# Shifted-window block and dynamic convolution on one core: the order of the projection's moving columns, its bias, and the place of the taps' product

## The chip, the cores and the metric

The kernel runs on 1 core of one Trainium2 chip, in one launch. The metric is the device time of an execution in microseconds (us); shown is the median of three runs. All tensors are float32. The engines are named as in the profile: PE is TensorE's matmul, PEld its weight load, DVE VectorE, ACT ScalarE, POOL GpSimd, SP the queue that issues most transfers.

## The reference

The input x is 16 images of 192 channels by 56 by 56. Layer 0 is a Swin block with windows of 7 by 7, a shift of 3 and 6 heads; layer 1 is a 3 by 3 depthwise convolution whose weights are computed from each image's channel means. Cut to what matters:

```
h = roll(ln(x), (-3, -3)); win = 7x7 windows of h            # 49 tokens each
q, k, v = split(win @ qkv_w + qkv_b)
attn = softmax(q * SCALE @ k.T + rel_bias + shift mask)
out = (attn @ v) @ proj_w + proj_b
x1 = x + roll(windows back to the image, (3, 3))
x2 = x1 + gelu(ln(x1) @ fc1_w + fc1_b) @ fc2_w + fc2_b
t  = relu(gamma * (mean(x2) @ w1.T - running_mean) * rsqrt(var + eps) + beta)
wt = (t @ w2.T + b2), masked to 4 of the 9 taps              # one set for each image and channel
y  = depthwise conv(x2, wt) + bias
```

## The kernel before

**Tiling.** An image is cut into four pairs of window rows. A unit s is one such pair, 14 pixel rows of one image: the upper window row lies on partitions 0 to 63 and the lower one on 64 to 127, and the 192 channels are G = 3 groups of 64. `rows(s)` is the unit's part of the tile x, [128, 3, 7 rows, 56 columns]. With 16 images there are 64 units. A window row has 8 windows of 49 tokens, UT = 392 tokens; HT = 196 is half of that, four windows.

**Stages.** The loop at L1364 makes one stage for each r and keeps several units in flight: values and scores of unit r, the weighted sum and `projection` of unit r-1, `first_layer` (FC1) of unit r-2, `second_layer` (FC2) of unit r-3, the two layer norms' `statistics` and `deviations`, and, where unit r-3 was the last of its image, `taps`. `conv` of an image follows in the stages after its taps, in six pieces. In steady state PE goes through a stage in this order, by lines: L654 values, L549 scores, L654 values, L690 weighted sum, L821 FC2, L746 and L732 projection, L469 queries and keys, L783 FC1, L318 statistics, and in every fourth stage L850, the taps' product.

**Order.** `Plan.add` records each operation with an engine, an estimated duration and the keys that it reads and writes. PE's operations keep the order in which they are added; `Plan.order` lists the other engines by earliest start and due time in its own estimates. Each engine then works through its list strictly in order, and so does SP. `bank()` hands out four PSUM tiles ps0 to ps3 in turn, so a product waits for the readers of the bank used four products earlier.

**Projection.** `broad` (L742) multiplies the heads' outputs o1 (128 channels) by `wp4`, `narrow` (L728) adds o2 (64 channels) by `wp2`. The copies at L717 and L719 leave o1 and o2 window by window, 49 tokens in a run. The moving operand is read as "p r n c": for each pixel row seven tokens of each of four windows. So the PSUM result is in pixel order, 28 columns to a row, and the sums of L770 read it in rows: for each group of channels one instruction for the first half (7 rows of 28), one for the second half without its last columns (7 of 25) and one for the 3 columns that wrap to the left edge, nine in all. Each is (psum + pbt) + x, with the projection's bias `pbt` as a scalar for each partition. `broad` uses the two column halves of the array, two matmuls side by side, and `narrow` all four quadrants. One matmul of the program is two records in the profile.

**Taps.** `taps(b)` (L835) sums up the means (`pooled`, L843), multiplies them by `w1t` with the 128 columns of a broadcast `pooled` as weights (L850, three matmuls), and on DVE makes the row of 48 (L861, L862), its products with `w2r` (L863), their sums and the bias of the taps (L876, L879).

The transfers that the text speaks of: `away` (L365) writes the inverse deviations to DRAM and L374 spreads them to `rb`; L454 (xs2) and L425 to L436 (xs1) on POOL scale x by rb for FC1 and for queries and keys; L282 loads x, L625 turns the attention shares, L948 stores y.

Of the kernel before, what the change touches and what calls it, by code (L numbers as in the profile page):

```python
# [9 lines left out]
AF = mybir.ActivationFunctionType  # L10
ALU = mybir.AluOpType
# [34 lines left out]
class Plan:  # L46
# [7 lines left out]
    def add(self, eng, dur, fn, reads=(), writes=(), lag=0.0, slack=60.0, by=None):  # L54
        i = len(self.ops)
        deps = set()
        reads, writes = flat(reads), flat(writes)
        for k in reads:
            if k in self.writer:
                deps.add(self.writer[k])  # L60
        for k in writes:
            if k in self.writer:
                deps.add(self.writer[k])
            deps.update(self.readers.get(k, ()))
        for k in reads:
            self.readers.setdefault(k, []).append(i)
        for k in writes:
            self.writer[k] = i
            self.readers[k] = []
        deps.discard(i)  # L70
        self.ops.append((eng, dur, fn, sorted(deps), lag, slack, by))
# [70 lines left out]
def tile_swin_then_dynamic_conv(  # L142
# [114 lines left out]
    def P(j):  # L257
        return slice(64 * j, 64 * j + 64)

    def X(s):  # L260

        b, u = divmod(s, NU)
        return [("x", b % 3, u, i) for i in range(3)]
# [409 lines left out]
    def weighted(s):  # L673
# [25 lines left out]
        for j in range(3):  # L699
# [8 lines left out]
            for i in range(4):  # L708
# [9 lines left out]
                else:  # L718
                    add("DVE", 0.56, lambda dst=dst, src=src: nc.vector.tensor_copy(dst, src), [k], [("o", j, i)])  # L719

    def projection(s):
        pf, kf = bank()
        pq, kq = bank()
        o1k = [("o", j, i) for j in range(2) for i in range(4)]
        o2k = [("o", 2, i) for i in range(4)]
        by_rows = "p n (r c) -> p r n c"

        def narrow():  # L728
            for m in range(G):
                for ab in range(2):  # L730
                    for i, p in ((0, pf), (1, pq)):
                        nc.tensor.matmul(  # L732
                            p[P(ab), m // 2, (m % 2) * HT : (m % 2) * HT + HT],
                            wp2[P(i), m * 64 : (m + 1) * 64],
                            o2[P(i), ab].rearrange(by_rows, c=WS),
                            start=False,
                            stop=True,
                            tile_position=(64 * i, 64 * ab),
                            skip_group_check=True,
                        )  # L740

        def broad():  # L742
            for i, p in ((0, pf), (1, pq)):
                for m in range(G):
                    for ab in range(2):
                        nc.tensor.matmul(  # L746
                            p[P(ab), m // 2, (m % 2) * HT : (m % 2) * HT + HT],
                            wp4[:, m * 64 : (m + 1) * 64],
                            o1[:, ab, 4 * i : 4 * i + 4].rearrange(by_rows, c=WS),
                            start=(m % 2 == 0),  # L750
                            stop=False,
                            tile_position=(0, 64 * ab),
                            skip_group_check=True,
                        )

        add("PE", 2.05, broad, o1k + ["wp"], [kf, kq])
        add("PE", 1.05, narrow, o2k + ["wp"], [kf, kq])
        xv = rows(s)
        hw = IMG // 2
        for p, k, c0, at, n, dur in (  # L760
            (pf, kf, 0, SHIFT, hw, 0.37),
            (pq, kq, 0, SHIFT + hw, hw - SHIFT, 0.35),
            (pq, kq, hw - SHIFT, 0, SHIFT, 0.2),
        ):
            for m in range(G):
                def go(p=p, c0=c0, at=at, n=n, m=m):
                    src = p[:, m // 2, (m % 2) * HT : (m % 2) * HT + HT]
                    src = src.rearrange("p (r c) -> p r c", c=hw)[:, :, c0 : c0 + n]
                    xs = xv[:, m, :, at : at + n]
                    nc.vector.scalar_tensor_tensor(  # L770
                        xs, src, pbt[:, m : m + 1], xs, ALU.add, ALU.add
                    )
                add("DVE", dur, go, [k, "pbt"], X(s))


    def first_layer(s):
# [58 lines left out]
    def taps(b):  # L835


        p, pk = bank()
        sl = b % 3
        add(  # L840
            "DVE",
            0.2,
            lambda: nc.vector.tensor_reduce(pooled, sums[b % 2], AX.X, ALU.add),  # L843
            [("sums", b % 2)],
            ["pooled"],
        )

        def product():
            for g in range(G):
                nc.tensor.matmul(  # L850
                    p[:, 0, 0:RED],
                    pooled[:, g : g + 1].broadcast_to([128, 128]),
                    w1t[:, g],
                    start=(g == 0),
                    stop=(g == G - 1),
                )

        add("PE", 0.3, product, ["pooled", "w1t"], [pk])

        def scale():  # L860
            nc.vector.tensor_tensor(trow, p[:, 0, 0:RED], bns, ALU.mult)  # L861
            nc.vector.tensor_tensor(trow, trow, bnb, ALU.add)  # L862
            nc.vector.scalar_tensor_tensor(  # L863
                prod,
                trow.rearrange("p (o r) -> p o r", o=1).broadcast_to([128, G * NTAP, RED]),
                0.0,
                w2r.rearrange("p g t r -> p (g t) r"),
                ALU.max,
                ALU.mult,
            )  # L870

        add("DVE", 1.2, scale, [pk, "bn", "w2r"], ["sq", "trow"])
        w = wt[b % 2].rearrange("p g t -> p (g t)")

        def fin():
            nc.vector.tensor_reduce(  # L876
                w.rearrange("p (k o) -> p k o", o=1), prod, AX.X, ALU.add
            )
            nc.vector.tensor_tensor(w, w, b2t.rearrange("p g t -> p (g t)"), ALU.add)  # L879

        add("DVE", 0.9, fin, ["sq", "b2t"], [("wt", b % 2)])
        t = xt[sl]
        for to, of, row in ((0, 1, LR), (1, 0, LR)):
            def go(to=to, of=of, row=row):
                nc.sync.dma_start(t[P(to), :, 0, :], t[P(of), :, row, :])
            add("SP", 0.65, go, X(b * NU + NU - 1), [("halo", sl, to)], lag=2.5)
# [474 lines left out]
    def has(s):  # L1361
        return 0 <= s < S

    for r in range(-2, S + 3):  # L1364
# [45 lines left out]
            turn_shares()  # L1410
        if has(r - 3):
            second_layer(r - 3)
        if has(r - 1):
            projection(r - 1)
            statistics(1, r - 1)
        if not early and has(r + 1):
            queries_keys(r + 1, (0, 1, 2))
        if has(r - 2):
# [2 lines left out]
            table("natural_log_exp_and_others")  # L1421
        if norms:
            deviations(norms)
        b, k = divmod(r - 3, NU)
        if k == NU - 1 and 0 <= b < B:
            taps(b)
        for b in range(B):
            k = r - (b * NU + NU + 3)
            if b == B - 1 and r == S + 2:
# [85 lines left out]
```

## Time and profile before

| what | value |
|---|---|
| median of 3 runs | 2835.39 us (2834.74 to 2842.21) |
| profiled execution: time | 2838.8 us |
| profiled execution: span | 2837.0 us |
| granted TensorE clock, mean | 0.99 |
| PE busy | 2771.9 us, 98% of the span |
| DVE, ACT, POOL busy | 1857.8, 1562.2, 1605.6 us |
| L746 (broad), L732 (narrow) busy | 153.1 us, 84.2 us |
| L770 (the sums) busy | 576 instructions, 156.1 us by the page |
| L850 (taps' product) busy | 13.9 us, 96 records |

Busy time of a matmul line is the time in which at least one of its records ran; single records overlap, so the mean of a record (347 ns for L746) is longer than its share. The start of a record minus the start of the one before it in the same part of the array is the pace. A releaser is the operation that ended a wait.

### The profile page before, as it was taken

What the parts mean: (1) busy time and instruction counts of PE and PEld (TensorE: products, weight loads), DVE (VectorE), ACT (ScalarE), POOL (GpSimd) and SP (SyncE); (2) the same over time, 40 slices, a digit from 0 to 9 for tenths busy, and PEclk for the clock granted to TensorE, in tenths of its full rate; (3) what the DMA queues carried; (4) which work ended last, traced back from release to release, by engine and by line L of the source; (5) the groups of instructions that cost most, each with busy time, mean ns of one, the idle gap of its engine ahead of it and who ended that gap; (6) DMA issues with size and microseconds to landing.
All of it is one profiled execution on the core that took longest, in us unless ns stands there. A gap on an engine that the chain in (4) does not pass through costs nothing.

```text
span 2837.0 us, 79158 instructions
## 1 busy us (share of the span) xinstructions
PE 2771.9 (98%) x34241; PEld 1718.4 (61%) x34241; DVE 1857.8 (65%) x3129; ACT 1562.2 (55%) x2338; POOL 1605.6 (57%) x1424
## 2 busy tenths in 40 slices
PE   7899999999999999999999999999999999999995
PEld 5566666666566666566566566566566566566552
DVE  5565675767677586675767666576675767667564
ACT  3545556556556456556556556456555556556452
POOL 5564565565565565565665565565665665665530
PEclk9899999999999999999999999999999999999997
DMA  6312232323313324233333313324133332313121
GB/s 128 81 28 48 54 76 60 78 63 73 84 37 79 74 56 90 47 73 70 73 67 73 82 37 81 72 58 90 41 74 74 73 69 67 81 40 76 43 52 50
DMA packets 122229, 189.32 MB, mean 67 GB/s; under 512 B 31208, under 2 KB 96664, under 8 KB 121880
## 3 DMA queue, kind: packets, MB, share of 16 engines
q1 hardware_dynamic: 117512, 184.24, 29.2%
q8 instruction: 269, 4.41, 0.7%
q10 hardware_dynamic: 4368, 0.02, 0.1%
q14 instruction: 80, 0.66, 0.1%
HBM read 66.81 MB, written 38.98 MB: 37 GB/s over the span
## 4 chain that ended last, share of the span: by engine, by line
PE 96%; DVE 1%; DMA 1%; issue 1%; POOL 0%; ACT 0%; SPq 0%; ACTq 0%; DVEq 0%; POOLq 0%
PE ps L783 27%; PE ps L821 27%; PE ps L469 14%; PE ps L654 9%; PE ps L746 5%; PE ps L690 5%; PE ps L549 4%; PE ps L732 3%; PE ps L318 2%; DVE hid L935 0%; PE ps L850 0%; POOL xs L425 0%; SPq L1236 0%; ACT q L506 0%; PE ps L1115 0%
## 5 line engine op out<-in xcount | busy, mean ns | idle before, releaser
L821 PE MATMUL ps<-hid,wf 128*64 128x392 f32 x4608 | 772.5, 494 | 0.8 <-ACT o L717 0.8
L783 PE MATMUL ps<-xs,wf 64*128 64x392 f32 x4608 | 771.2, 490 | 2.1 <-POOL xs L454 2.1
L783 PEld LDWEIGHTS ps<-xs,wf 64*128 64x128 f32 x4608 | 446.5, 187 | 315.9 <-POOL xs L454 3.6
L821 PEld LDWEIGHTS ps<-hid,wf 128*64 128x64 f32 x4608 | 327.2, 137 | 411.2 <-issue 386.2
L302 POOL TENSOR_TENSOR fold<-sq 128x392 f32<-128x392 f32 x128 | 131.5, 1027 | 577.9 <-PE ps L318 509.7
L795 ACT ACTIVATE hid<-ps,b1f 128x784 f32<-128x784 f32 x384 | 341.5, 913 | 170.7 <-PE ps L783 168.6
L590 POOL TENSOR_TENSOR e<-e,top 128x784 f32<-128x784 f32 x192 | 306.2, 1610 | 216.4 <-DVE top L585 216.4
L469 PE MATMUL ps<-xs,wqkv 64*128 64x392 f32 x2304 | 404.0, 502 | 10.6 <-POOL xs L436 9.7
L935 DVE SCALAR_TENSOR_TENSOR y<-x,wt,y 128x770 f32<-128x770 f32 x270 | 329.5, 1234 | 86.1 <-ACT y L911 49.6
L482 ACT ACTIVATE q<-ps,qbs 128x400 f32<-128x400 f32 (+1 forms) x128 | 68.4, 589 | 493.6 <-PE ps L469 493.6
L608 POOL TENSOR_TENSOR e<-e,tot 128x784 f32<-128x784 f32 x192 | 307.3, 1614 | 49.3 <-DVE tot L603 47.1
L469 PEld LDWEIGHTS ps<-xs,wqkv 64*128 64x128 f32 x2304 | 221.6, 190 | 173.5 <-issue 18.6
L654 PE MATMUL ps<-wqkv,xs 64*64 64x192 f32 x6144 | 276.4, 325 | 0.0
L302 POOL TENSOR_TENSOR fold<-x 128x392 f32<-128x392 f32 x128 | 131.5, 1027 | 254.1 <-PE ps L318 166.7
L454 POOL TENSOR_TENSOR xs<-x,rb 128x392 f32<-128x392 f32 x192 | 236.9, 1261 | 30.1 <-DMA rb<-rsd 30.1
L717 ACT COPY o<-ps 32x392 f32<-32x392 f32 x512 | 246.5, 481 | 9.0 <-PE ps L690 2.7
L619 DVE STREAM_TRANSPOSE tt<-e 128x512 f32<-128x512 f32 x384 | 246.3, 685 | 5.1 <-POOL e L608 3.6
L654 PEld LDWEIGHTS ps<-wqkv,xs 64*64 64x64 f32 x6144 | 224.6, 133 | 29.0 <-issue 15.4
L575 DVE TENSOR_TENSOR e<-ps,bt 128x784 f32<-128x784 f32 x192 | 175.1, 968 | 99.2 <-PE ps L549 99.0
L770 DVE SCALAR_TENSOR_TENSOR x<-ps,pbt,x 128x196 f32<-128x196 f32 (+2 forms) x576 | 156.1, 344 | 96.5 <-PE ps L732 93.0
L602 DVE TENSOR_REDUCE tot<-e 128x16 f32<-128x784 f32 x192 | 180.4, 939 | 34.4 <-ACT e L597 34.3
L425 POOL TENSOR_TENSOR xs<-x,rb 128x343 f32<-128x343 f32 x192 | 186.5, 999 | 24.4 <-PE ps L654 17.4
(105 smaller groups left out, 3236.9 us busy)
## 6 DMA issues: line engine op xcount, KB each, us to landing
pt<-tt SPq DMA_DIRECT2D x256, 192.0 KB
x<-in_x_dram SPq DMA_DIRECT2D x112, 294.0 KB
out_dram<-y SPq DMA_DIRECT2D x135, 196.0 KB
pt<-tt SPq DMA_DIRECT2D x256, 96.0 KB
rb<-rsd SPq DMA_DIRECT2D x118, 196.0 KB
out_dram<-y SPq DMA_DIRECT2D x45, 154.0 KB
x<-in_x_dram SPq DMA_DIRECT2D x16, 168.0 KB
pt<-tt SPq DMA_DIRECT2D x128, 12.0 KB
```

The lines of the kernel that those rows point to most:

```text
L302: nc.gpsimd.tensor_tensor(f, src[:, 0], src[:, 1], ALU.add)
L454: nc.gpsimd.tensor_tensor(xs2[:, g], xv[:, g], rb[:, 1], ALU.mult)
L469: nc.tensor.matmul(p[:, ab, 0:UT], lhs_qk(ab, g, i), d[P(ab), g, 0:UT], start=(g == 0), stop=(g == G - 1), tile_position=(64 * ab, 0),)
L590: nc.gpsimd.tensor_tensor(ev, ev, top[j].broadcast_to([128, 16, N]), ALU.subtract)
L608: nc.gpsimd.tensor_tensor(ev, ev, tot[j].broadcast_to([128, 16, N]), ALU.mult)
L619: nc.vector.transpose(tt[:, kb, 16 * j : 16 * j + 16], src)
L654: nc.tensor.matmul(p[P(w % 2), ab, i * DIM : (i + 1) * DIM], d[P(ab), g, w * N : w * N + 64], wqkv[P(ab), g, 2 * DIM :], start=(g == 0), s ...
L717: add("ACT", 0.5, lambda dst=dst, src=src: nc.scalar.copy(dst, src), [k], [("o", j, i)])
L783: nc.tensor.matmul(p[:, ab, 0:UT], wf1[P(ab), g, f * 128 : (f + 1) * 128], xs2[P(ab), g], start=(g == 0), stop=(g == G - 1), tile_position ...
L795: nc.scalar.activation(hid[:, f], p[:, :, 0:UT], AF.Gelu, bias=b1f[:, f : f + 1])
L821: nc.tensor.matmul(p[P(ab), 0, 0:UT], wf2[:, f, g * 64 : (g + 1) * 64], hid[:, f, ab], start=(f == 0), stop=(f == NFC - 1), tile_position= ...
L935: nc.vector.scalar_tensor_tensor(dst, s_, w[:, g, t : t + 1], dst, ALU.mult, ALU.add)
```

## The change

Three things change in the code.

1. Both products of the projection read o1 and o2 flat, window by window as the copies left them. PSUM then holds windows of 49 tokens, and the sums are cut by windows: for each group four windows (7 rows of 28 pixels), three windows (7 of 21), and the last window in two parts (7 of 4 and 7 of 3). That is twelve instructions for nine, each a `tensor_tensor` of PSUM and x.
2. The bias is no longer in the sums. `biased_rows` adds it to x beforehand, in three ACT instructions of 128x392 for each unit.
3. `projection` yields between broad and narrow, and in the stages that have taps, `taps(b)` is added there; it was added after `deviations` at the end of the stage. Its product is made in column halves: six matmuls of 64 weight columns, 12 records, for three of 128 columns, 6 records.

```diff
+    def biased_rows(s):
+        xv = rows(s).rearrange("p g r c -> p g (r c)")
+        for m in range(G):
+            add("ACT", 0.53, lambda m=m: nc.scalar.activation(
+                xv[:, m], xv[:, m], AF.Identity, bias=pbt[:, m : m + 1]), ["pbt"], X(s))
...
-                            o2[P(i), ab].rearrange(by_rows, c=WS),
+                            o2[P(i), ab].rearrange(flat_),
...
-                            o1[:, ab, 4 * i : 4 * i + 4].rearrange(by_rows, c=WS),
+                            o1[:, ab, 4 * i : 4 * i + 4].rearrange(flat_),
...
         add("PE", 2.05, broad, o1k + ["wp"], [kf, kq])
+        yield
         add("PE", 1.05, narrow, o2k + ["wp"], [kf, kq])
...
-            (pf, kf, 0, SHIFT, hw, 0.37),
-            (pq, kq, 0, SHIFT + hw, hw - SHIFT, 0.35),
-            (pq, kq, hw - SHIFT, 0, SHIFT, 0.2),
+            (pf, kf, 0, SHIFT, nw, 0, WS, 0.37),
+            (pq, kq, 0, SHIFT + nw * WS, nw - 1, 0, WS, 0.33),
+            (pq, kq, nw - 1, IMG - WS + SHIFT, 1, 0, WS - SHIFT, 0.18),
+            (pq, kq, nw - 1, 0, 1, WS - SHIFT, SHIFT, 0.18),
...
-                    nc.vector.scalar_tensor_tensor(
-                        xs, src, pbt[:, m : m + 1], xs, ALU.add, ALU.add
-                    )
+                    src = p[:, m // 2, (m % 2) * HT : (m % 2) * HT + HT]
+                    src = src.rearrange("p (w r c) -> p r w c", r=WS, c=WS)
+                    src = src[:, :, w : w + n, c0 : c0 + nc_]
+                    xs = xv[:, m, :, at : at + n * nc_].rearrange("p r (w c) -> p r w c", c=nc_)
+                    nc.vector.tensor_tensor(xs, src, xs, ALU.add)
...
-                    pooled[:, g : g + 1].broadcast_to([128, 128]),
+                        pooled[:, g : g + 1].broadcast_to([128, 64]),
...
+                        tile_position=(0, 64 * ab),
...
+        weighing = k == NU - 1 and 0 <= b < B
         if has(r - 1):
-            projection(r - 1)
+            biased_rows(r - 1)
+            for _ in projection(r - 1):
+                if weighing:
+                    taps(b)
             statistics(1, r - 1)
+        elif weighing:
+            taps(b)
...
-        if k == NU - 1 and 0 <= b < B:
-            taps(b)
```

## Prediction before the run

> **What bounds the kernel.** I read the page first, then the chain of work that ended last in a stretch of the steady state, then windows, then single lines.
>
> ```profile
> PE 2771.9 (98%) x34241; PEld 1718.4 (61%) x34241; DVE 1857.8 (65%) x3129; ACT 1562.2 (55%) x2338; POOL 1605.6 (57%) x1424
> ```
>
> PE is the bound and nothing else is near. The chain between 1000 and 1190 us (start, length, what), one ordinary stage and the end of the next:
>
> ```profile
> 1086.93 12.00 PE ps L821 x72
> 1098.93 2.17 PE ps L746 x24
> 1101.10 1.24 PE ps L732 x24
> 1102.34 6.13 PE ps L469 x36
> 1108.46 11.85 PE ps L783 x72
> 1120.31 0.80 PE ps L318 x16
> 1121.11 2.11 PE ps L654 x48
> ...
> 1162.64 0.80 PE ps L318 x16
> 1163.44 0.80 PE ps L850 x6
> 1164.24 2.11 PE ps L654 x48
> ```
>
> The chain is PE from end to end: what PE saves in a stage is saved from the time, as long as no new wait appears. The windows from one start of L746 to the next give 42.33 us for the ordinary stage and 43.11 for the one with the taps:
>
> ```profile
> 1098.76:1141.09 42.33, 42.33 (x535) 26.17 (x533) 24.08 (x43) 22.56 (x34) 25.90 (x25) 1.00 0.42 92
> 1141.09:1184.20 43.11, 43.11 (x540) 26.91 (x538) 28.12 (x49) 24.36 (x36) 24.11 (x23) 1.00 0.19 41
> ```
>
> So the taps' product costs 0.79 us, in 15 stages; the sixteenth product is in the tail. Starts of L746 taken one after the other show 42.33 in nearly all other stages. Only the stage after the taps varies (42.33 to 43.80, 8.2 us in all, by waits inside L690 that the chain calls "issue").
>
> **Part 1, the flat order, on the path.** The chain gives the pace. L821: 36 pairs in 12.00 us, 0.333 us for 392 columns. L654: 12 sets of four in 1.95 us, 0.1625 us for 192. Both read their moving operand in one run, 0.85 ns a column, so 196 columns should pace at 0.166. L318 has exactly that shape (196 columns in one run) and the starts of its records lie 0.166 us apart. L746 takes 2.17/12 = 0.181, and both its starts and L732's are 0.180 apart. The records differ in the same way:
>
> ```profile
> L746 PE MATMUL ps<-o,wp x1536: 340/341/589, 90.1 to 2752.7; 128*64 128x196 f32 x192
> L318 PE MATMUL ps<-fold,blk x984: 329/329/353, 101.7 to 2766.8; 128*32 128x196 f32 x197
> ```
>
> (min, median, max ns.) L690 reads runs of 25 and its starts, 0.086 us for 100 columns, show no loss; L746 and L732 alone read runs of 7. I put the 14.2 ns down to those runs. There are 12 paces in broad and 6 in narrow: 18 x 14.2 = 256 ns a stage. The first two of the 64 stages wait for POOL and not for PE; 62 x 0.256 = **-15.9 us**. Bounds: 0, if the loss comes from something that stays, and -15.9.
>
> **Part 2, sums and bias, beside PE.** Each ACT addition is 128x392 and 0.53 us (L409 has that shape and time), three are 1.6 us a stage. They stand behind the table load at about 6 us before L746, in a hole: ACT had nothing from 1094.1 to 1104.6 but one 0.34 us instruction at 1098.4. Cover gone, they would hold up the sums, not PE. In the two stages after the taps a convolution's L911 stands ahead of them in ACT's list; its y buffer was given to L948 some 20 us earlier.
>
> DVE's sums:
>
> ```profile
> L770 DVE SCALAR_TENSOR_TENSOR x<-ps,pbt,x 128x196 f32<-128x196 f32 x192 | 69.0, 414 | 96.5 <-PE ps L732 93.0 <-issue 3.4
> L770 DVE SCALAR_TENSOR_TENSOR x<-ps,pbt,x 128x21 f32<-128x21 f32 x192 | 33.4, 228 | 0.0
> L339 DVE TENSOR_TENSOR m<-ps,m 128x196 f32<-128x196 f32 x59 | 21.2, 360 | 215.6 <-ACT m L332 215.6
> ```
>
> Starts of L770 are 0.33 apart for 196 elements and 0.146 for 21. A tensor_tensor of the same size is 54 ns shorter (L339), so I take 0.28, 0.225, 0.10 and 0.095 for 196, 147, 28 and 21: 3 x 0.70 = 2.1 us in twelve instructions, against 2.35 in nine. Bounds: 2.1, and 3.9 at twice the price for each element. In an ordinary stage both ends are hidden. The third product of queries and keys needs the first three sums (its bank), starts 4.1 us after narrow, and they take at most 1.7; FC1's first needs all twelve 6 us after narrow. POOL's folds wait for the sums, but its last one ends some 10 us ahead of L318. Priced at nothing.
>
> [...]
>
> **Part 3, the taps.** Removed: 15 x 0.79 = -11.9 us. Added, for six pairs of 48 columns with 64 weight columns: L850 starts 0.112 apart with 128 weight columns, so half of that, 0.056, is bounded by the weights; the 48 columns alone need 0.042 (0.85 ns each). Six are 0.34, and the step to L732 costs about what it did. I take 0.38; bounds 0.25 and 0.75 (no overlap of the two halves' loads). PE's wait for `pooled` is covered: in the taps stage L843 ends 1.05 us after L746's start and broad lasts 2.0. Queued behind that wait are L732 and all the rest of PE.
>
> The price is on DVE. In the changed order L861, L862 and L863 stand ahead of the twelve sums, and the taps take a bank before queries and keys, so now the second product needs the first three sums, the third all twelve. L862 is not a 0.2 us instruction there:
>
> ```profile
> L862 DVE TENSOR_TENSOR trow<-trow,bnb x16: 207/772/777, 310.7 to 2809.2; 128x48 f32<-128x48 f32 x16
> ```
>
> ```profile
> 1142.21 2.98 POOL L608 TENSOR_TENSOR e<-e,tot 128x784 f32<-128x784 f32 x2
> ```
>
> It is 207 ns in two of 16 and some 770 in fourteen, where it ends 0.07 us after the POOL instruction in flight (1164.59 to 1165.36; L304 ended at 1165.30). It has two SBUF inputs; the sums have one in PSUM, and L770 is 414 whether POOL runs or not. In all 15 taps stages POOL's second L608 runs from 2.6 to 4.1 us (4.4 in one) after L746's start. In that time scale: the product ends at 2.55, L861 starts at 2.66 and L862 at 2.90; it is held to 4.2; L863 starts at 4.3, the sums at 4.98 (0.675 after it, as before). Three sums end at 4.98 + 0.56 + 0.36 = 5.9, PE sees it at 5.97. PE: L732 from 2.48, L469 from 3.64 (0.28 after narrow's last set, as before), its first product 2.08: ready at 5.72. Wait 0.25, or 0.40 with L770's paces: I take **0.3**. All twelve are done by 7.3, the third product comes at 8.0. Sum for 15 stages: 15 x (-0.79 + 0.38 + 0.3) = **-1.6 us**. Bounds: -8 (no wait, 0.25), +13 (sums at twice the price, wait 1.25).
>
> What moves along: L876 and L879 (0.9 us) come after the sums and push L493, whose bank FC1's third product needs at about 13.7; it is through by 10.6. L295 writes sq, which L863 and L876 use, so it waits to about 8.3, and the folds of it end near 13, with L318 at 21.6. Four transposes (L619) fall behind L525, some 1.2 us later than now, and with them the ten transfers of L625; these landed some 6 us before L690. The two halo copies (L885) keep their place in SP's list. Six L935 of the convolution follow in the same stage (1.02 each alone) and end near 22.5; L339 behind them is due at 22.8, and its rb has 5 us to spare.
>
> [...]
>
> **The rest.** The last taps product, behind FC2, is 0.3 to 0.4 shorter; at the start the eight bias additions fit into ACT's idle 6.5 us before 97.85, one more delays a fold that PE already waits 0.37 for, and the final norm's chain (PE waits 2.1 us for L454) sees sums of about the same length: +0.4 together. The waits in L690 come 1.0 to 1.7 us after the end of a 16 KB transfer of the instruction queue; stores and loads move to other stages in SP's list and PE's code shifts by 12 records an image, so they may fall to 0 or double: 0, bounds -8 and +8.
>
> **Sum**: -15.9 - 1.6 + 0.4 = -17.1. From the profiled execution's 2838.8 (span 2837.0 and 1.8 around it) that is 2821.7; that execution lay 3.4 above the median of the runs, 2835.4, so the forecast is **2818 us**, 0.6% faster. The three runs differ by 0.26%, so 0.3% (8.5 us) is about what tells a change from none.
>
> **Rivals.**
> A. L608 runs a little earlier, and L862 falls between two POOL instructions: no hold, the taps gain 0.41 in full, 2835.4 - 15.9 - 6.1 + 0.4 = 2814. For: L608's first ends at 2.6, 0.3 from L862. Against: in 15 of 15 the second is then in flight.
> B. The sums in runs of 7 cost twice for each element: the wait in the taps stages is 1.25 for 0.3, 2818 + 15 x 0.95 = 2832, and the gain is within the measurement. [...]
> C. The change does not do what it says to the pace: 0.180 stays, because four strides of PSUM or the weights set it. 2834. Against: L318 and L654 with the same columns and quadrants.
> D. Slower. In SP's new list, in the stage ahead of an ordinary one of every four, four loads of x stand between `away` and the two spreads of `rb`. They issue in 4 x 0.7 = 2.8 us, in the 2.7 that SP waits for rsd anyway; but their packets go ahead of rb's, and two such loads took 3.3 us of the rings. So rb lands perhaps 3 to 6 us later than its usual 10 us before L746. L425 needs it 4 us before; PE stalls once it lands later than about 1 us before, that is 9 us late, and each us beyond costs 15. To be slower by 0.3% it takes 1.7 us of stall in each, 10.7 us late: 2844 or more. Against: 6.6 us of transfers at most.
>
> **Chances.** Forecast 0.52, A 0.15, B 0.16, C 0.08, D 0.09. Faster: the forecast, A, and half of B (a price in between), 0.75; same: C and the other half, 0.16; slower: 0.09. The range runs from A without the L690 waits to B: 2808 to 2832; D and most of C lie outside. The forecast's own range is 2811 to 2826.
>
> **What the changed profile would show.** Right: L746 and L732 records at 329 ns or less, L746 1.99 us and L732 about 1.15 in the chain, ordinary stages 42.07, taps stages near 42.76 with DVE's sums as releaser of L469. L862 still near or above 0.77, ended by L608. The 196-element sum near 360 ns. Wrong: 340 ns records (C), PE waits behind xs1 in ordinary stages (D), sums above 500 ns or waits of L469 above 0.6 us in taps stages (B).

## The result, and the profile after

The changed kernel takes 2821.23 us (median of six runs, 2816.53 to 2827.20), the kernel before in the same session 2838.22 (six runs, 2834.74 to 2842.21): a ratio of 0.9943, 95% interval 0.9928 to 0.9957. In a second session, beside other kernels, it took 2826.77 (2825.22 to 2829.80) against 2836.69: 0.9964, 0.9951 to 0.9977. So it is faster by 0.4 to 0.6%. The profiled execution took 2820.61 us, its span is 2818.8, 18.2 shorter than before.

The page after:

```profile
PE 2754.4 (98%) x34337; PEld 1716.8 (61%) x34337; DVE 1833.4 (65%) x3321; ACT 1671.2 (59%) x2530; POOL 1570.5 (56%) x1424
```

PE is busy 17.5 us less and still bounds the kernel. ACT has 109 us more (105.4 of it the bias additions, L728), and nothing of that shows in the chain of the stages. A taps stage in the chain of work that ended last (start, length, what):

```profile
1302.99 1.99 PE ps L760 x24
1304.98 0.33 PE ps L867 x12
1305.32 1.16 PE ps L746 x24
1306.47 2.18 PE ps L469 x12
1308.65 0.03 issue
1308.67 4.22 PE ps L469 x24
```

L760 is broad (2.17 before), L746 narrow (1.24 before), L867 the taps' product (0.79 before, elsewhere). L469 takes 6.43 us from 1306.47 to its end, 6.13 in the stages around it: 0.30 us more, which I put down to a wait for the sums (the run with the row in PSUM, below, shows it). The windows of the ordinary stage ahead of it, and of this one:

```profile
1260.93:1302.99 42.06, 42.06 (x535) 26.20 (x533) 21.41 (x43) 25.81 (x40) 23.84 (x23) 1.00 0.19 40
1302.99:1345.70 42.71, 42.68 (x548) 26.65 (x546) 34.18 (x59) 28.03 (x41) 23.43 (x23) 1.00 0.27 60
```

42.06 and 42.71, for 42.33 and 43.11. The records of broad by line (min, median and max in ns), which were 340/341/589 before:

```profile
L760 PE MATMUL ps<-o,wp x1536: 329/329/589, 88.7 to 2738.6; 128*64 128x196 f32 x192
```

DVE's sums by form (busy time, mean ns of one, idle time before), and the row that L862 added before and L880 adds now:

```profile
L788 DVE TENSOR_TENSOR x<-ps,x 128x196 f32<-128x196 f32 x192 | 57.4, 354 | 69.3 <-PE ps L746 69.3
L788 DVE TENSOR_TENSOR x<-ps,x 128x147 f32<-128x147 f32 x192 | 47.1, 300 | 0.0
L788 DVE TENSOR_TENSOR x<-ps,x 128x28 f32<-128x28 f32 x192 | 23.2, 176 | 0.0
L788 DVE TENSOR_TENSOR x<-ps,x 128x21 f32<-128x21 f32 x192 | 21.8, 169 | 0.0
L880 DVE TENSOR_TENSOR trow<-trow,bnb 128x48 f32<-128x48 f32 x16 | 21.3, 1333 | 0.6
```

The sums cost 354 to 169 ns each. The addition of 48 elements takes 1333 ns, which DVE's timeline and POOL's of that taps stage explain (start, length):

```profile
1305.61 1.41 DVE L880 TENSOR_TENSOR trow<-trow,bnb 128x48 f32<-128x48 f32 x1
1307.05 0.76 DVE L881 SCALAR_TENSOR_TENSOR sq<-trow,w2r 128x576 f32<-128x576 f32 x1
1307.73 2.08 DVE L788 TENSOR_TENSOR x<-ps,x 128x196 f32<-128x196 f32 x12
```

```profile
1304.00 2.95 POOL L608 TENSOR_TENSOR e<-e,tot 128x784 f32<-128x784 f32 x2
```

L880 ends at 1307.02, 0.07 us after POOL's L608 (1306.95). The twelve sums end 6.99 us after broad's start at 1302.82, 2.08 us for all.

**Where the 18.2 us came from.** Starts of broad, stage by stage, before and after:

| part of the span | before | after | difference |
|---|---|---|---|
| start to the fourth stage | 202.6 | 200.7 | -1.8 (197.7 to 205.4 in the profiles of all kernels here: no step of the change) |
| 60 stages | 2548.1 | 2536.1 | -12.0 |
| from the last stage's start to the end | 86.4 | 82.0 | -4.3 |

The 60 stages fall into three terms. The shortest ordinary stage went from 42.33 to 42.06, about -0.265 in each: -15.9. A taps stage stood 0.79 above the ordinary one and now stands 0.60 above it (shortest of each; 0.64 in the median): 15 x -0.19 = -2.9. What the stages take above the shortest of their kind went from 8.4 to 15.1 us: +6.7. By position in the image it lay before in the stage after the taps alone (8.3); now 6.5 lie there, 7.3 in the next one, 1.3 in the other two. The waits of PE, from 200 to 2640 us (line, releaser, us in total, times, longest):

```profile
PE ps L690 <- issue: 3.6, 5, 1.7
PE ps L837 <- issue: 2.5, 2, 1.9
PE ps L837 <- ACT o L717: 0.8, 1, 0.8
PE ps L654 <- issue: 0.4, 2, 0.3
PE ps L549 <- issue: 0.4, 1, 0.4
```

Before there was one such line of "issue" (L690, 4.2 us). The view counts less than the stages show, 6.9 us of "issue" against 15.1; I take it that the ends of the matmuls, which the profile models, cover part of a stall. I call these waits for code: read packet by packet, each of the long ones ends 1.2 to 1.7 us after the end of a 16 KB transfer of the instruction queue. That cause is an inference at this point; the last experiments test it.

The tail gained what nobody had counted. Before, the chain has the last unit's FC1 wait for rb (first fence), and FC1 itself then runs at the pace of L454's scaling; after (second fence) PE goes straight through:

```profile
2776.79 3.17 DMA rb<-rsd
...
2781.18 13.80 PE ps L783 x72
```

```profile
2752.95 12.00 PE ps L837 x72
2764.95 12.05 PE ps L799 x72
```

In the chain of before the spread L374 of rb stands behind two stores L948, and these behind L935 of the fifteenth image's convolution. With the taps half a stage earlier, that convolution is out of the way. A wait of 2.1 us goes, FC1 is 1.75 shorter and the last taps product 0.3 (0.88 to 0.58): 4.2 of the 4.3. One profile of each is little for a tail, but the other kernels bear it out: it takes 84.8 to 86.4 us in the profiles with the taps at their old place and 81.9 to 82.2 in those with the early taps, so the gain is some 3 to 4 us.

### The profile page after: what moved, and what is told of

Same layout as the page of the kernel before. It is cut to its first block, busy times and chain, and to the rows that moved or that the text cites. A ratio compares the mean times of both kernels' runs of the same rounds, so it can differ in the third digit from the quotient of the medians.

```text
span 2818.8 us, 79628 instructions
## 1 busy us (share of the span) xinstructions
PE 2754.4 (98%) x34337; PEld 1716.8 (61%) x34337; DVE 1833.4 (65%) x3321; ACT 1671.2 (59%) x2530; POOL 1570.5 (56%) x1424
## 4 chain that ended last, share of the span: by engine, by line
PE 96%; DVE 1%; ACT 1%; POOL 1%; issue 1%; DMA 0%; ACTq 0%; SPq 0%; DVEq 0%; POOLq 0%
PE ps L837 27%; PE ps L799 27%; PE ps L469 14%; PE ps L654 9%; PE ps L760 5%; PE ps L690 5%; PE ps L549 5%; PE ps L746 3%; PE ps L318 2%; DVE hid L953 0%; POOL xs L425 0%; PE ps L867 0%; ACT o L717 0%; PE ps L383 0%; DVE trow L880 0%
## 5 line engine op out<-in xcount | busy, mean ns | idle before, releaser
L837 PE MATMUL ps<-hid,wf 128*64 128x392 f32 x4608 | 773.4, 494 | 3.3 <-issue 2.5
L837 PEld LDWEIGHTS ps<-hid,wf 128*64 128x64 f32 x4608 | 327.8, 137 | 413.8 <-issue 381.4
L590 POOL TENSOR_TENSOR e<-e,top 128x784 f32<-128x784 f32 x192 | 285.6, 1503 | 253.8 <-DVE top L585 253.8
L469 PE MATMUL ps<-xs,wqkv 64*128 64x392 f32 x2304 | 408.5, 504 | 11.0 <-POOL xs L436 9.7
L953 DVE SCALAR_TENSOR_TENSOR y<-x,wt,y 128x770 f32<-128x770 f32 x270 | 302.8, 1136 | 85.7 <-ACT y L946 63.3
L469 PEld LDWEIGHTS ps<-xs,wqkv 64*128 64x128 f32 x2304 | 220.3, 190 | 178.1 <-issue 21.8
L608 POOL TENSOR_TENSOR e<-e,tot 128x784 f32<-128x784 f32 x192 | 290.6, 1524 | 56.8 <-DVE tot L603 54.7
L654 PE MATMUL ps<-wqkv,xs 64*64 64x192 f32 x6144 | 278.1, 325 | 0.6 <-issue 0.4
L454 POOL TENSOR_TENSOR xs<-x,rb 128x392 f32<-128x392 f32 x192 | 249.6, 1328 | 25.4 <-DMA rb<-rsd 25.4
L654 PEld LDWEIGHTS ps<-wqkv,xs 64*64 64x64 f32 x6144 | 224.6, 133 | 35.1 <-issue 22.1
L339 DVE TENSOR_TENSOR m<-ps,m 128x196 f32<-128x196 f32 (+1 forms) x64 | 23.2, 362 | 306.4 <-ACT m L332 306.3
L728 ACT ACTIVATE x<-x,pbt 128x392 f32<-128x392 f32 x192 | 105.4, 612 | 191.2 <-POOL xs L436 191.2
L666 ACT COPY v<-ps 128x768 f32<-128x768 f32 x128 | 102.3, 799 | 194.3 <-PE ps L654 194.3
```

What stands on the lines that cost most here:

```text
L454: nc.gpsimd.tensor_tensor(xs2[:, g], xv[:, g], rb[:, 1], ALU.mult)
L469: nc.tensor.matmul(p[:, ab, 0:UT], lhs_qk(ab, g, i), d[P(ab), g, 0:UT], start=(g == 0), stop=(g == G - 1), tile_position=(64 * ab, 0),)
L590: nc.gpsimd.tensor_tensor(ev, ev, top[j].broadcast_to([128, 16, N]), ALU.subtract)
L608: nc.gpsimd.tensor_tensor(ev, ev, tot[j].broadcast_to([128, 16, N]), ALU.mult)
L654: nc.tensor.matmul(p[P(w % 2), ab, i * DIM : (i + 1) * DIM], d[P(ab), g, w * N : w * N + 64], wqkv[P(ab), g, 2 * DIM :], start=(g == 0), s ...
L837: nc.tensor.matmul(p[P(ab), 0, 0:UT], wf2[:, f, g * 64 : (g + 1) * 64], hid[:, f, ab], start=(f == 0), stop=(f == NFC - 1), tile_position= ...
```

## The experiments

One number is used throughout: **excess**, what 58 stages of the steady state take above the shortest of their kind (four kinds by position in the image: the taps stage and the first, second and third after it). Stage lengths are the shortest of the kind. Each row's stages come from one profiled execution; the median is that of all its runs.

| kernel | ordinary | taps | excess (taps, first, second, third) | median us | ratio, 95% interval |
|---|---|---|---|---|---|
| before | 42.33 | 43.12 | 8.4 (0, 8.3, 0.1, 0) | 2838.22 | |
| after | 42.06 | 42.66 | 15.1 (1.0, 6.5, 7.3, 0.3) | 2821.23 | 0.9943, 0.9928 to 0.9957 |
| after, again | 42.06 | 42.40 once, else 42.69 | 23.4 (5.6, 8.0, 8.9, 0.9) | 2826.77 | 0.9964, 0.9951 to 0.9977 |
| flat order alone | 42.06 | 42.86 | 6.0 (0, 5.7, 0.1, 0.1) | 2822.08 | 0.9944, 0.9929 to 0.9960 |
| taps at their old place | 42.06 | 42.55 | 8.5 (0.4, 8.0, 0, 0) | 2819.48 | 0.9937, 0.9921 to 0.9954 |
| row of 48 in PSUM | 42.06 | 42.40 | 22.3 (1.8, 8.1, 11.9, 0.6) | 2821.61 | 0.9943, 0.9927 to 0.9958 |
| taps alone | 42.33 | 42.73 once, else 42.85 | 17.9 (3.1, 8.0, 6.4, 0.5) | 2839.14, one run | (before 2841.35, one run) |
| broad in runs of 2, narrow of 49 | 42.17 | 42.66 | 19.6 (1.6, 8.2, 9.6, 0.2) | 2830.36, one run | (the same) |
| broad in runs of 14, narrow of 4 | 42.08 | 42.65 | 21.4 (1.2, 8.6, 11.0, 0.5) | 2829.93, one run | (the same) |
| fewer stores | 42.06 | 42.66 | 15.7 (1.0, 14.2, 0.5, 0) | 2823.36, one run | (the same) |
| old place, again | 42.06 | 42.55 | 9.9 (0.3, 9.6, 0, 0) | 2820.74 | 0.9937, 0.9921 to 0.9954 |
| old place, loads spread | 42.06 | 42.55 | 16.8 (1.7, 8.8, 4.1, 2.3) | 2825.21 | 0.9953, 0.9938 to 0.9969 |
| row in PSUM, loads spread | 42.06 | 42.44 | 21.6 (8.5, 9.1, 2.2, 1.8) | 2824.90 | 0.9955, 0.9940 to 0.9970 |
| row in PSUM, transfers behind rb | 42.06 | 42.40 | 0.03 | 2805.08 | 0.9882, 0.9865 to 0.9898 |

In "after, again" one taps stage has no wait for the sums: its addition L880 took 0.80 us, where the other fourteen of the loop took 1.40 to 1.45. The shortest stage is thus of another sort than the rest, and 13 x 0.29 = 3.8 us of the 23.4 are that wait; 19.6 is the figure to compare.

### The changed kernel again, and the change taken apart

The first four ran on one chip and share the runs of the kernel before (2836.69). The changed kernel, without an edit:

> The changed kernel once more, so that the others of this call have it beside them on the same chip. Every theory: 0.994 of the kernel before; ordinary stages 42.07 us from one start of the broad product to the next, taps stages 42.70.

Measured: 2826.77. The stages are those of the first session, and the excess is 19.6 for 15.1 once the wait for the sums is taken out. The two profiled executions are 7.0 us apart (spans of 2825.9 and 2818.8): 4.6 of it lies in the stages, in waits for code, and 2.5 in the start. The two medians are 5.5 us apart, so a kernel is best compared with the changed one of its own session.

The flat order with the bias ahead, and the taps as they were in place and form:

```diff
-                for ab in range(2):
-                    nc.tensor.matmul(
-                        p[P(ab), 0, 0:RED],
-                        pooled[:, g : g + 1].broadcast_to([128, 64]),
...
+                nc.tensor.matmul(
+                    p[:, 0, 0:RED],
+                    pooled[:, g : g + 1].broadcast_to([128, 128]),
...
             for _ in projection(r - 1):
-                if weighing:
-                    taps(b)
+                pass
...
+        if weighing:
+            taps(b)
         for b in range(B):
```

> Flat order, sums by blocks and the bias ahead; the taps as before (end of the stage, three matmuls of 128 weight columns). Theory (the runs of 7 set the projection's pace, the rest is hidden): ordinary stages 42.07, taps stages 42.07 + 0.79 = 42.86, in all 2838.2 - 15.9 = about 2822, that is nearly all of the gain. Rival (the place of the taps carries the gain): ordinary stages 42.33, no gain over the kernel before.

Measured: 2822.08, stages of 42.06 and 42.86 (0.80 for the taps), excess 6.0. The flat order alone gives the whole of the gain. Beside it on the same chip the changed kernel is 4.7 us slower, and the runs of the two don't overlap (2817.55 to 2824.57, 2825.22 to 2829.80); in the first session the changed kernel took 2821.23. So the taps' part adds no gain that these runs can tell, and may cost up to some 5 us.

The 12 records, but the taps at the end of the stage, as before:

```diff
             for _ in projection(r - 1):
-                if weighing:
-                    taps(b)
+                pass
...
+        if weighing:
+            taps(b)
         for b in range(B):
```

> The changed kernel with the taps, still in 12 records, added at the end of the stage as before. Theory (the form saves PE time by itself; the new place pays with a wait of PE for the sums): the product costs 0.79 less six times half of 0.112 = about 0.45, no wait of the queries' product for the sums, taps stages 42.52 against 42.70, 2.7 us less over 15 stages. Rival (the place is what saves, since the array is not switched twice): taps stages 42.75 or more, no better than the changed kernel.

Measured: 2819.48, 7.3 less than the changed kernel beside it, where 2.7 were expected (2820.74 in a later session). The taps stage is 42.55, 0.31 under the one with the old form and 0.11 under the changed kernel's, and the excess stays at 8.5, in the stage after the taps. So the column halves are worth 0.31 us a taps stage, and the early place by itself costs the taps stages 0.11 to 0.15 each and some 5 to 11 us of excess. The tail is its return: 85.9 us from the last stage's start here, 82.0 in the changed kernel.

The changed kernel with the row of 48 in PSUM, so that its addition has one SBUF input:

```diff
-    trow = sb("trow", 128, RED)
...
         def scale():
+            trow = p[:, 1, 0:RED]
...
-        add("DVE", 1.2, scale, [pk, "bn", "w2r"], ["sq", "trow"])
+        add("DVE", 1.2, scale, ["bn", "w2r"], [pk, "sq"])
```

> The changed kernel with the taps' row of 48 kept in PSUM, so that its addition and its product with w2r have one SBUF input each. Theory (DVE's instruction with two SBUF inputs is held by the GpSimd instruction in flight, and that holds the sums and then PE): the addition takes about 0.2 us where it took 1.33, PE does not wait for the sums, taps stages 42.07 + 0.33 = 42.40, 4.5 us less than the changed kernel over 15 stages. Rival (the addition waits for its own input, or for anything but SBUF): it stays at 1.3 and the taps stages at 42.70.

Measured, the addition by line (min, median, max ns), and the chain in a taps stage (lines are one lower in this kernel: L759 is broad, L866 the taps' product, L468 queries and keys):

```profile
L880 DVE TENSOR_TENSOR ps<-ps,bnb x16: 216/216/217, 287.6 to 2794.2; 128x48 f32<-128x48 f32 x16
```

```profile
1307.01 1.99 PE ps L759 x24
1309.00 0.33 PE ps L866 x12
1309.34 1.16 PE ps L745 x24
1310.49 6.13 PE ps L468 x36
```

216 ns in all sixteen for 1333 on average, L468 without a wait, and a taps stage of 42.40: the addition was held by POOL as long as its row lay in SBUF, and the 0.30 us of PE was that hold. The time is 2821.61: 5.2 us less than the changed kernel of the same session, where 4.5 were expected, but no less than the changed kernel of the first session (2821.23). The profiles show why a time alone doesn't settle it. The excess is 22.3, 11.9 of it in the second stage after the taps, and the 60 stages together are 1.4 us shorter than in the changed kernel beside it and 3.2 longer than in that of the first session. From here on the waits for code were the open question.

The taps' part alone, on the kernel before (its sums, its bias, its moving columns; the edit is shown against the changed kernel):

```diff
-            biased_rows(r - 1)
...
-                            o1[:, ab, 4 * i : 4 * i + 4].rearrange(flat_),
+                            o1[:, ab, 4 * i : 4 * i + 4].rearrange(by_rows, c=WS),
...
-                    nc.vector.tensor_tensor(xs, src, xs, ALU.add)
+                    nc.vector.scalar_tensor_tensor(
+                        xs, src, pbt[:, m : m + 1], xs, ALU.add, ALU.add
+                    )
```

> The kernel before with the taps between the projection's two products, in 12 records, alone. Theory: ordinary stages stay at 42.33; the product costs 0.33 in place of 0.79; the row's addition is held by GpSimd as in the changed kernel, the sums start 4.9 us after the broad product, three of them end at 6.0, and PE, ready at 3.51 + 0.33 + 2.08 = 5.92, waits 0.1 to 0.2: taps stages 42.8 (43.12 before), about 5 us in all. Rival (no hold): 42.66. Rival (the taps carry the whole gain): taps stages near 42.0.

Measured: one time of 2839.14 beside 2841.35; ordinary stages 42.33, taps stages 42.73 and mostly 42.9, excess 17.9, of it 6.4 in the second stage after the taps. The extra waits come with the early taps, with or without the flat order, and so does the shorter tail (82.2 us).

### What the runs of seven cost

Two kernels keep the changed one's order of work and read the same 196 elements in other runs; their projections are made of the wrong columns. Broad in 98 runs of 2, narrow in 4 runs of 49:

```diff
-                            o2[P(i), ab].rearrange(flat_),
+                            o2[P(i), ab].rearrange(flat_).rearrange("p (a b c) -> p b a c", a=2, b=2),
...
-                            o1[:, ab, 4 * i : 4 * i + 4].rearrange(flat_),
+                            o1[:, ab, 4 * i : 4 * i + 4].rearrange(flat_).rearrange("p (a b c) -> p b a c", a=2, b=49),
```

> The changed kernel with the moving columns in another order (the sums then add the wrong columns): the broad product reads 98 runs of 2 elements, all starting on an even element; the narrow one 4 runs of 49. Theory 1 (a break in the run costs by itself, 14.2 ns over 28 breaks or 0.5 ns each): paces 0.166 + 98 x 0.0005 = 0.215 and 0.168 us. Theory 2 (elements are read in aligned pairs, and only a run that splits a pair costs; a run of 7 takes 4 pairs for 3.5): 0.166 and 0.167. Theory 3 (the number of dimensions of the pattern costs): 0.180 and 0.180.

Broad in 14 runs of 14, narrow in 49 runs of 4, by the same edit with other sizes (`a=2, b=7` and `a=7, b=7`):

> As the one before it, with 14 runs of 14 in the broad product and 49 runs of 4 in the narrow one (wrong columns again). Theory 1 (each break 0.5 ns): 0.173 and 0.190 us. Theory 2 (aligned pairs): 0.166 and 0.166. Theory 3 (dimensions): 0.180 and 0.180.

Measured, in the chain of each: broad and narrow in one ordinary stage, first with 98 runs of 2 and 4 of 49, then with 14 of 14 and 49 of 4:

```profile
1264.06 2.08 PE ps L760 x24
1266.14 1.17 PE ps L746 x24
```

```profile
1265.55 2.00 PE ps L760 x24
1267.55 1.16 PE ps L746 x24
```

Starts of records, per 196 columns, against one run at 0.166 us: 28 runs of 7 cost 14.2 ns (the kernel before), 4 runs of 49 cost 2 to 3, 14 runs of 14 cost 1 to 3, 49 runs of 4 nothing, 98 runs of 2 cost 7. A price for each break falls: 49 runs of 4 have more breaks than 28 of 7, and none of the cost. A price for the number of dimensions falls too, since these patterns have as many as the old one. What is left is the odd length: some 0.5 ns for each odd run (14.2/28, 2.5/4). That is the price which fits, and not a mechanism that is shown: runs of odd length also start on odd elements half the time, and no run here parts the two. L690's four runs of 25 cost less, 1.3 ns (0.0859 us against 100/196 of 0.1658). The 7 ns of the runs of 2 this doesn't explain, and it stays open.

### What makes PE wait for code

In the changed kernel, the stage after a taps stage shows such a wait in the chain:

```profile
1369.72 2.00 PE ps L549 x91
1371.72 0.38 issue
1372.10 0.30 PE ps L549 x3
```

and SP's queue at that time (start, length, what):

```profile
1358.66 6.55 SPq L625 DMA_DIRECT2D pt<-tt  x10
1365.33 1.40 SPq L282 DMA_DIRECT2D x<-in_x_dram  x2
1366.77 4.38 SPq L966 DMA_DIRECT2D out_dram<-y  x5
1371.37 0.61 SPq L365 DMA_DIRECT2D rsd<-rs  x1
1373.10 2.09 SPq L374 DMA_DIRECT2D rb<-rsd  x2
```

Loads of x and stores of y stand between L625's ten transfers and the two spreads of rb. They move data just as PE goes through L654, L549 and L690 from 1367.6 on, its small matmuls: 288 records in some 8 us, where L837 takes 12 us for 72. In the 8 us ahead of the wait the rings moved 1.6 MB.

First, the stores taken out: images 1 to 14 are not stored, and their outputs stay unwritten.

```diff
-            add("SP", 0.65, go, [yk], [], lag=12.0)
+            if b == B - 1 or b == 0:
+                add("SP", 0.65, go, [yk], [], lag=12.0)
```

> The changed kernel without the stores of the images 1 to 14 (their outputs are not written; the convolution is still computed). Theory (PE's waits inside the weighted sum are for its code, whose transfers share the rings with stores and loads): the excess of the stages over 42.07 and 42.66, 13.9 us in the changed kernel's profile, falls below 5 us. Rival (the waits have nothing to do with the stores): about 14 us again.

Measured: one time of 2823.36, excess 15.7. The second stage after the taps lost its waits (0.5 for 7.3) and the first gained as much (14.2 for 6.5); the loads of x now issue there together. The stores are not the cause by themselves.

Next, the loads. In the kernels so far up to seven of an image's nine load transfers issue together, when its tile comes free. Here each unit's loads issue in a stage of its own. Beside the kernel with the taps at their old place, again:

> The kernel with the taps at their old place once more, as the neighbour of the two runs below. Its stages alone give 42.07 and 42.54; with 6 to 9 us of waits for code, all in the stage that carries the bunched loads and stores: 2817 to 2822 us.

```diff
-        if has(r + 3) and r >= 1:
-            load(r + 3)
+        if r == 1:
+            load(4)
+        if has(r + 4) and r >= 1:
+            load(r + 4, reads=[("hid", 3)] if r > 8 else [])
```

> Taps at their old place, and the loads of x spread: each unit's two or three load transfers are issued in a stage of its own, behind L625's ten, where before seven of an image's nine stood together. Theory that waits for code come from bunched transfers: the densest stretch falls from about 1.5 MB in 8 us to 1 or less, the waits above the shortest stages fall from 6-9 us to under 3, and the time by 5 us against the kernel without it, 2812 to 2816. Rival, that only the place of PE's code counts (the waits come where small matmuls use it up fastest, whatever the transfers do): waits stay at 6 to 9, 2817 to 2822. Rival, that any transfer beside L690 and L654 counts: the waits spread to all four kinds of stage and their sum stays or grows.

> Taps at their new place with the row of 48 in PSUM, and the loads of x spread in the same way. Without the spreading this kernel had stages of 42.07 and 42.39 and 22 us of waits for code: 2821.6. Theory of bunched transfers: the waits fall below 6 and the shorter taps stages show at last, 2806 to 2811 us, the best of all. Rival of the code's place alone: waits stay near 20, 2820 to 2825. Rival of any transfer: the waits move to other kinds of stage, 10 to 25 in sum, 2812 to 2825.

Measured: 2825.21 and 2824.90. The waits lie in all four kinds of stage; their sum went up in the one (9.9 to 16.8) and stayed in the other (22.3 to 21.6, in another session). With the loads spread and the taps at the old place, PE's waits from 200 to 2640 us are

```profile
PE ps L690 <- issue: 4.1, 7, 1.3
PE ps L654 <- issue: 2.6, 6, 0.8
PE ps L837 <- issue: 0.2, 1, 0.2
```

for 5.6 us in L690 alone without the spreading. That the bunch matters falls. With the loads spread, 13 stages of the third kind have two loads and no store behind L625's ten, and 2 of them have a wait (1.3 and 0.9 us over the shortest): so few are enough, and now more stages have some. They don't bring a wait each time: with the taps at their old place the second stage after them has six stores there and no wait. The idea that was left is that their place matters. The last kernel puts loads and stores behind the spreads of rb in SP's list, in the row-in-PSUM kernel with spread loads:

```diff
-            load(r + 4, reads=[("hid", 3)] if r > 8 else [])
+            load(r + 4, reads=[("rb", 0, 0)] if r > 8 else [])
...
-            add("SP", 0.65, go, [yk], [], lag=12.0)
+            add("SP", 0.65, go, [yk, ("rb", 0, 0)] if b < B - 2 else [yk], [], lag=12.0)
```

> The kernel with the row of 48 in PSUM, its loads of x one unit a stage, and now loads and stores held in SP's list until both spreads of rb, so that they run some 30 us after L760's start, beside the second half of the weighted sum and FC2, and no longer between L625's ten transfers and rb. Theory that a fetch of PE's code is late when transfers of x or y run in or right behind L625's ten: without them there the waits fall from 22 to under 6 us, and with stages of 42.07 and 42.40 the time is 2804 to 2811, the best of all. Rival, that any transfer beside the small products counts, wherever: waits stay at 10 to 25 us, perhaps in other parts of the stage (L837, L760), 2812 to 2825. Rival, that the later loads or stores hold up others (POOL's folds of x, the convolution's buffers): waits of PE behind POOL or DVE appear, 2815 and more.

Measured: 2805.08 us (2803.41 to 2806.25), 0.9882 of the kernel before, the fastest of all. PE has no wait at all between 200 and 2640 us, and the excess is 0.03 (21.6 in its neighbour, row in PSUM with loads spread, which differs from it in these two lines alone). SP's queue in the stage after a taps stage, and the two PE lines that had waited longest for "issue" (1.9 and 5.2 us in the row-in-PSUM kernel with the transfers where they were):

```profile
1354.27 6.56 SPq L624 DMA_DIRECT2D pt<-tt  x10
1366.98 0.57 SPq L364 DMA_DIRECT2D rsd<-rs  x1
1368.71 1.36 SPq L373 DMA_DIRECT2D rb<-rsd  x2
1370.12 2.71 SPq L966 DMA_DIRECT2D out_dram<-y  x4
1372.87 2.76 SPq L281 DMA_DIRECT2D x<-in_x_dram  x3
```

```profile
L836 PE MATMUL ps<-hid,wf 128*64 128x392 f32 x4608 | 772.5, 494 | 0.0
L689 PE MATMUL ps<-pt,v 64*64 64x100 f32 x6144 | 144.0, 244 | 3.9 <-ACT q L505 3.9
```

The same bytes move, beginning with the end of the small products (L689 runs from 1369.1 to 1371.4) and then beside FC2. (The 3.9 us left over are in the start of the program.)

That these are waits for code, the traces show by count. Number the records of PE and PEld in the order of their starts, and count the 16 KB transfers of the larger instruction queue (q8) as they end. In the 14 profiles there are 163 waits of PE over 0.1 us between 200 and 2640 us, none of them in the last kernel. Every one ends at the record with the number 256 n + 193, where n is the count of transfers that have ended, and 1.2 to 1.7 us after the end of the n-th. So PE's code comes in blocks of 256 records, and PE stands still at the edge of a block.

Of the 163 waits, 162 lie in stages in which SP issues at least one load of x or store of y between L625's ten and rb's second spread; the other is 0.35 us long.

So what is shown: the waits for code, 6 to 22 us in all kernels but this one, go with transfers of x and y that run between L625's and rb's, and are gone when these are moved behind rb. Read packet by packet, the rings moved this much in the 8 us before a fetch that starts 25 to 32 us after broad (median, largest), with the excess beside it: taps at the old place 0.40 and 1.6 MB, 9.9 us; changed kernel 1.16 and 1.7, 15.1; row in PSUM 1.20 and 1.7, 22.3; transfers behind rb 0.28 and 0.9, 0.03. The median alone doesn't set the excess: the kernel with fewer stores has 0.40 and 1.7 MB, and 15.7 us.

The traces also show where in the fetch the time goes. PE's small products use up a block in some 3.6 us. For the blocks that PE uses up in under 4.5 us, the next transfer starts 0.25 us (median, 1.1 at most) after PE's first record of the block before it in the kernel with the transfers behind rb, 0.60 (2.8) in the changed kernel and 1.09 (2.1) in the one with row in PSUM and loads spread. The transfer itself takes 1.13, 1.04 and 1.19 us. So it starts late and is not slow. What makes it start late is not shown.

## Why the prediction was right, point by point

The forecast of 2818 was met within 3.2 us in the first session and 8.8 in the second, inside the range of 2808 to 2832 both times (the second lies 0.8 outside the forecast's own 2811 to 2826). In the first session the kernel gained 17.0 us over the kernel before, and the sum had said 17.1; that closeness is luck: two errors cancel, +6.7 us of waits in the stages and some -5 in the start and the tail. The three runs of before that the forecast stood on also had a median 2.8 us below the six.

- **Part 1, the pace: right.** Predicted 0.166 us and 329 ns records, ordinary stages of 42.07 and 1.99 us for L746 (now L760). Measured 329 ns, 42.06, 1.99 and 1.16. The term of -15.9 for 62 stages measured -15.9 for 60. That runs of seven set the pace was inferred; the runs of other lengths bear it out, as a price that goes with odd runs; why is open.
- **Part 2, sums and bias: right.** Predicted 0.36 us for the largest and 2.1 for twelve; 0.354 and 2.08. The bias took 0.61 us for 0.53, and no wait of PE between 200 and 2640 us names it. Read from PSUM in runs of 3, 4 and 7, the sums cost 1.06 ns an element from 21 to 196 elements (169 to 354 ns). The kernel before had it too: L770 took 228 ns for 21 elements in runs of 3, within 15 ns of the line through its 390 for 175 and 414 for 196.
- **Part 3, the taps: right in its mechanism.** Predicted for the taps stage: product 0.38, wait of PE 0.3, hold of L862 (now L880) until POOL's L608 ends at 4.2, sums at 4.98. Measured 0.33, 0.30, 4.2 and 4.9; the stage 42.70 in the median for 42.76. The term of -1.6 measured -2.9 at the shortest stages. The hold was shown by taking it away: 1333 ns on average with the row in SBUF, 216 with it in PSUM. In 15 of the 16 additions of the changed kernel's profile POOL's L608 was in flight, and each ended 0.06 to 0.07 us after it; the sixteenth had no POOL instruction beside it and took 0.21 us.
- **The waits in L690: wrong in size.** "0, bounds -8 and +8" measured +6.7, and some +11 in the second session, outside its bounds. This is the term of the sum that was mis-sized. The prediction had tied them to the 16 KB transfers, had seen that stores and loads move in SP's list, and then put the term at zero because it could fall or rise. The row to weigh was at hand: the waits of before lie in the one stage that has loads and stores behind L625, and the change gave another stage of four the same.
- **"The rest", +0.4: wrong in sign.** The final norm's chain was taken as it was ("PE waits 2.1 us for L454"). The taps' new place moved the fifteenth image's convolution and with it the stores ahead of rb in SP's list, and the wait went: the tail measured -4.3, 0.3 of it the pace, and is 3 to 4 us shorter in all kernels with the early taps. The start's -1.8 is within its scatter.
- **Rivals.** A's 0.30 us a taps stage came true with the row in PSUM, by another way, and in one taps stage of the changed kernel's second session (42.40); with the row in PSUM the time was 5.2 us below the changed kernel of its session and level with that of the first. B fell with the 354 ns, C with the 329. D's delay came: in one stage of four rb lands 5.6 us before L760 instead of 10.2, 4.6 later where 3 to 6 were expected, and PE doesn't stall behind it.

## What to carry to other kernels

Give a float32 moving operand on TensorE long or even runs: 28 runs of 7 cost 14.2 ns in 180 for each matmul, 14 runs of 14 cost 1 to 3, 49 runs of 4 nothing (though 98 runs of 2 cost 7), and no profile line names that cost; two lines with equal columns and unequal pace do. Where PE is busy from end to end, look at stages one by one against the shortest of their kind: what lies above it, here 6 to 22 us, can be larger than the edit under study, and moving transfers away from the stretch with the smallest matmuls was worth as much as the whole change (2824.90 to 2805.08 us). Compare a variant with the changed kernel of its own session, and term by term in the profiles: the kernel without the hold of L880 gained 5.2 us by the one session and nothing by the other, while its taps stages are 0.3 us shorter by both.

## What the runs showed of the hardware

- A fetch of PE's code in 16 KB transfers is not always hidden. With the transfers behind rb, and 0.28 MB moved in the 8 us before the fetch (median), it was: excess 0.03 us over 58 stages. With small matmuls on PE and, mostly, 1.2 to 1.7 MB moved in the 8 us before the fetch it was 0.1 to 2.6 us at a time, in 163 waits. PE's code comes in blocks of 256 records of PE and PEld, and every wait ends at the edge of one.
- Spreading the same transfers thinner over the stages made the waits no fewer (9.9 to 16.8 us in one kernel, 22.3 to 21.6 in the other); moving them 6 to 11 us later within the stage ended them.
- A taps product of six matmuls with 64 weight columns in column halves takes 0.33 us, three with 128 columns 0.79: the pair of halves starts every 0.058 us, about half the 0.112 of the full width.
